# Two scan layers on one Trainium2 core: y kept in DRAM in the order of PSUM's channel blocks, and the second direction of an orientation added by an accumulating DMA

## The chip, the cores and the metric

The kernel runs on one core of a Trainium2 chip. The metric is device time in microseconds (us), the median of three executions. The core has five engines that run beside each other, each with its own queue in program order: PE (matrix multiply; loads of its weights are shown as PEld), DVE (vector), ACT (activations and copies), POOL (GpSimd) and SP (which here only issues DMAs). They meet through semaphores.

## The reference: what is computed

An image batch x of 8 x 64 x 64 x 192 passes two layers; each adds to x the result of a selective scan over the group-normalised x. In one layer:

- `xz = x . in_proj`, split into `xx` and `z`, 384 channels each; `xx` passes a 3 x 3 depthwise convolution and a silu: `xs`, read as a line of L = 4096 positions.
- K directions: layer 0 has two (the line forward and backward, row by row), layer 1 four (row by row and column by column, each forward and backward). For each direction `x_dbl = x_proj . xs` gives dt, B and C; `delta = softplus(dt_proj . dt + bias)`.
- The scan, with 16 states n for each channel d: `h[t] = exp(delta[t] * A) * h[t-1] + delta[t] * xs[t] * B[t]`, `y[t] = sum over n of h[t] * C[t]`; then `y += xs * Ds`.
- The y of all directions are added, each at its own place of the image. Then a layer norm over the channels, times gelu(z) or silu(z), times `out_proj`, plus x.

All of it is in float32.

## The kernel before, in words

Channels stand on the 128 partitions in three tiles (`DT`), so 384 = 3 x 128, and each tile has four blocks of 32 channels (`Q`). The line of an image is cut into 8 chunks of 512 positions (`T`). Each layer has two stages. `front` (L205) makes the normalised x, the convolution and the projections and stores `xs` to DRAM (xcd, row order; xcd_col, column order; xtd, transposed). `scans` (L511) does the rest, and the change lies in it.

**Steps and slots.** `scans` runs over steps: for each image b, each direction k, each chunk c (from the last to the first for a backward direction). Layer 0 has 128 steps, layer 1 has 256. A step has 24 slots (`NSL`): 8 pairs of states m times 3 channel tiles dt. In a slot PE makes `hb` = delta xs B (`inject`, L728) in PSUM, ACT makes `da` = exp(delta A) (`decay`, L745), DVE scans the two states (`scan`, L772, two instructions of 512 positions) into `h`, and POOL multiplies h by C into `hc` (L773). `cr`, which holds C spread over the partitions, is loaded by SP (`load_c`, L714; three buffers). When the three tiles of a pair are done, PE adds `hc` into `py`, a PSUM tile of 128 x 3 x 512, by `reduce` (L780).

**How py is summed.** `block_diag` (L147) multiplies by a 32 x 32 diagonal, four blocks for each tile: block i of tile dt goes to block (i + dt) mod 4 of the partitions. The twelve small multiplications of one state thus use twelve different 32 x 32 places of PE's array and run at the same time. So py holds the channels of tile dt rotated by dt blocks. (In the trace each such multiplication shows as two records, 24 for one state.)

**The order.** It is written out by hand: `at(i, s, f)` puts a helper f at slot s of step i, and slots beyond 24 fall into the next step. `L0_SLOTS` and `L1_SLOTS` (L50, L95) hold the places. Within a slot the scan comes first, then the helpers, then `inject` for two slots later and `decay` for four slots later. Nothing reorders the instructions afterwards.

**y between the directions**, which the change touches:

- k = 0 (first direction): `load_y` at slot 6 loads `xs` (from xcd or xcd_col), and `add_y` (slot 12 in layer 0, 13 in layer 1) adds it to py, times Ds.
- k whose predecessor has the same orientation (layer 0: k = 1; layer 1: k = 1, by columns, and k = 3, by rows): `load_y` loads the y so far from `yrow` or `ycol` in DRAM, and `add_y` adds it by a diagonal of ones.
- layer 1, k = 2, the change from columns to rows: `load_turned` at slots 8 to 19 (L797) loads the chunk's eight rows out of `ycol` in 12 DMAs (3 tiles x 4 parts, runs of 8 numbers, 32 bytes), and `add_y` stands at slot 26.
- `keep_y` at slot 29, which is slot 5 of the next step, copies py to SBUF on ACT (L821) and stores it with five DMAs of SP (L825, L827). Tile 0 goes as it is; tiles 1 and 2 go in two parts each, which turns their blocks back into channel order.

The loaded y, its turned form and the copy of py share one SBUF buffer, called "y" (pool s1, one buffer): each waits for the reader of the one before.

**The final part** (`f_...`) of a finished chunk: `f_load_x` (L836) loads x into `xr`, `f_load` (L850) loads y from `yrow` into `yc`, both at slot 6; then norm, gate (`f_gate`, L871), mean and variance, scale, product with the gate on POOL (`f_times`, L944), output projection (`f_out`, L950). For the images before the last it is spread over the steps of the next image: a chunk every second step in layer 0, every fourth in layer 1. In the last image it comes at once, in the step after the chunk's last direction (`L0_LAST`, `L1_LAST`); there `f_mean` (L888) reads yc from slot 11 (layer 1) or 13 (layer 0) on.

POOL's queue holds the 24 multiplications of a step, two small products for the start of a chunk (`enter`, L665), and the three products of the gate where a chunk is finished. SP's queue holds all loads and stores of the scan stage.

Of the kernel before, what the change touches and what calls it, by code (L numbers as in the profile page):

```python
# [8 lines left out]
F32 = mybir.dt.float32  # L9
AF = mybir.ActivationFunctionType  # L10
ALU = mybir.AluOpType
# [4 lines left out]
P = 128  # L16
B = 8
H = 64
# [5 lines left out]
D = 384  # L24
DT = 3
NS = 16
T = 512
NCH = L // T
RB = T // W
Q = 32  # L30
# [480 lines left out]
def scans(tc, name, x_src, x_dst, xcd, xcd_col, xtd, xdd, t, dirs, rank, row_b, gate, slots, last, consts, dram):  # L511
# [5 lines left out]
    nc = tc.nc  # L517
    ident, mask, grp, mean_w, all_w, eps_gn, eps_ln = consts
    yrow, ycol, cscr, dgd = dram
# [6 lines left out]
    def tiles(a):  # L526
        return a.rearrange("(t p) l -> p t l", p=P)
# [7 lines left out]
    def line(src, c):  # L535
        return src[:, :, c * T : (c + 1) * T]

    steps = []
# [6 lines left out]
    with tc.tile_pool(name=f"{name}_s1", bufs=1) as s1, tc.tile_pool(  # L545
        name=f"{name}_s2", bufs=2
    ) as s2, tc.tile_pool(name=f"{name}_psy", bufs=1, space=PSUM) as psy, tc.tile_pool(
        name=f"{name}_psh", bufs=2, space=PSUM
# [4 lines left out]
        def at(i, s, f, *a):  # L553
            todo.setdefault(i * NSL + s, []).append((f, a))

        live = {}
# [232 lines left out]
        def load_y(i):  # L789

            b, k, cols, rev, ci, c = steps[i]
            y_t = s1.tile([P, DT, T], F32, name="y")
            src = (xcd_col if cols else xcd) if k == 0 else (ycol if cols else yrow)
            nc.sync.dma_start(out=y_t, in_=line(tiles(src[b if k == 0 else b % 2]), c))
            live[i]["y"] = y_t

        def load_turned(i, j):  # L797

            b, k, cols, rev, ci, c = steps[i]
            if j == 0:  # L800
                live[i]["yt"] = s1.tile([P, DT, T], F32, name="y")
                live[i]["y"] = live[i]["yt"].rearrange("p t (w h) -> p t h w", h=RB)
            dt, q = divmod(j, 4)
            cs = slice(q * W // 4, (q + 1) * W // 4)
            nc.sync.dma_start(
                out=live[i]["yt"].rearrange("p t (w h) -> p t w h", h=RB)[:, dt, cs],
                in_=tiles(ycol[b % 2])[:, dt].rearrange("p (w h) -> p w h", h=H)[
                    :, cs, c * RB : (c + 1) * RB
                ],
            )  # L810

        def add_y(i):
            k = steps[i][1]
# [3 lines left out]

        def keep_y(i):
            b, k, cols, rev, ci, c = steps[i]
            y_o = s1.tile([P, DT, T], F32, name="y")  # L820
            nc.scalar.copy(y_o, live[i]["py"])  # L821
            yv = tiles((ycol if cols else yrow)[b % 2])
            for dt in range(DT):
                yd, e = yv[:, dt, c * T : (c + 1) * T], dt * Q
                nc.sync.dma_start(out=yd[: P - e], in_=y_o[e:, dt])  # L825
                if e:
                    nc.sync.dma_start(out=yd[P - e :], in_=y_o[:e, dt])  # L827
            del live[i]


# [137 lines left out]
        def thrice(i, s, f, *a):  # L968
            for p, q in enumerate(s):
                at(i, q, f, *a, p)  # L970

        for i in range(N):
            j = i - 1
            live[i] = {}
            at(j, -3, load_xt, i)
            if xdd is None:
                at(j, -8, load_x, i)
                thrice(j, slots["x_proj"], x_proj, i)
                at(j, slots["x_dbl"], x_dbl, i)
            else:  # L980
                at(j, -4, load_xdbl, i)
            at(j, slots["turn_b"], turn_b, i)
            at(j, slots["keep_b"], keep_b, i)
            for dt in range(DT):
                for f in dt_proj, dt_bias, turn_delta, make_dut:
                    at(j, slots[f.__name__][dt], f, i, dt)
            at(j, slots["softplus"], dt_softplus, i)
            at(j, slots["softplus"] + 1, first_decays, i)
            at(j, 14, enter, i, 0)
            at(j, NSL + 1, enter, i, 1)  # L990
            at(i, -12, load_b, i, 0)
            at(i, 0, load_b, i, 1)
            for m in range(NP):
                at(i, 3 * m - 6, load_c, i, m)
                at(i, 3 * m + 3, carry, i, m)
                for n in range(2):
                    at(i, 3 * m + slots["reduce"][n], reduce, i, m, n)
            b, k, cols, rev, ci, c = steps[i]
            if k and dirs[k - 1][0] != cols:
                for j in range(4 * DT):  # L1000
                    at(i, 8 + j, load_turned, i, j)
                at(i, slots["add_turned"], add_y, i)
            else:
                at(i, 6, load_y, i)
                at(i, slots["add_y"], add_y, i)
            at(i, slots["keep_y"], keep_y, i)

        e = 0
        for b in range(B - 1):
            for c in range(NCH):  # L1010
                e = max(e + K, (b + 1) * K * NCH - NCH + c + 1)
# [19 lines left out]
        for c in range(NCH):  # L1031
            b, e, own = B - 1, N - NCH + c + 1, last
# [34 lines left out]
            for r, fs in enumerate(  # L1067
# [3 lines left out]
                    (dt_proj, turn_b, turn_delta, f_gate, f_mean, f_sum, f_all, f_out, x_proj),  # L1071
                    (reduce, add_y),
                    (load_b, load_c, load_turned),
                )
            )
            for f in fs
        }
        with tc.manual_schedule(engines=ENGINES):
            g = min(todo)
            while todo:  # L1080
                i, s = divmod(g, NSL)
# [11 lines left out]
def vss_layer(tc, name, x_src, x_dst, w, dirs, rank, row_b, gate, slots, last, consts, dram):  # L1093

    with ExitStack() as ctx:
        xcd, xcd_col, xtd, xdd, *dram = dram
        if any(cols for cols, rev in dirs):
            xdd = None
        else:
            xcd_col = None  # L1100
        t = load_weights(tc, ctx, name, w, len(dirs), rank, row_b + 2 * NS, consts[1])
        clear = dram[-1] if xcd_col is None else ()
        front(tc, name, x_src, xcd, xcd_col, xtd, xdd, w["in_proj"][:, :D], t, clear, consts)
        scans(tc, name, x_src, x_dst, xcd, xcd_col, xtd, xdd, t, dirs, rank, row_b, gate, slots, last, consts, dram)
# [99 lines left out]
```

## Time and profile before

| | |
|---|---|
| three runs | 25205.74, 25212.66, 25232.09 us; median 25212.66 |
| profiled execution | span 25231.1 us (the page gives no other time of it), 18.4 above the median and within the three runs |
| scans of layer 0 | 961 to 8928 us |
| scans of layer 1 | 9865 to 25182 us |
| busy share | PE 95%, DVE 93%, POOL 88%, ACT 77% |
| DMA | 4141 MB, 164 GB/s in the mean; SP's queue 61.7% of 16 engines |
| chain that ended last | PE 50%, DVE 25%, ACT 19%, issue 5%, DMA 1% |

Busy time says how long an engine had an instruction running; PE's is modelled for pipelined multiplications. The groups list for each source line the busy time, the mean of one instruction in ns and the idle time of the engine just before it with the releaser that ended most of it. The stretches view gives busy times between two times; here stretches are single steps. The timeline lists instructions in order of time, consecutive ones of a group merged, with the idle time before them in brackets.

### The profile page before, as it was taken

The numbers are of one execution on the slowest core, as the hardware profiler recorded it, in microseconds if no ns is written. First come the engines' busy times: TensorE is split into PE (matmuls) and PEld (weight loads), VectorE is DVE, ScalarE is ACT, GpSimd is POOL, SyncE is SP. The second block draws the span as 40 slices with busy tenths as digits, with TensorE's granted clock in tenths as the row PEclk, the third lists the DMA queues.
The fourth block names the chain that finished last, engine by engine and source line by source line (L and its number), as shares of the span: only waits on it lengthen the run. The fifth ranks groups of instructions, "written<-read, shape, count | busy, mean of one in ns | idle before, by whom it ended". The sixth has DMA issues, their size and how long they took to land.

```text
span 25231.1 us, 794569 instructions
## 1 busy us (share of the span) xinstructions
PE 24024.7 (95%) x340032; PEld 13528.4 (54%) x340032; DVE 23345.8 (93%) x22142; ACT 19452.6 (77%) x37140; POOL 22144.2 (88%) x10287
## 2 busy tenths in 40 slices
PE   9999999999999999999999999999999999999999
PEld 4555555555555544555555555555555555555554
DVE  7899999999999777999999999999999999999998
ACT  5677788778878767777777777777777777777777
POOL 0499999999999713999999999999999999999998
PEclk9999999999999999999999999999999999999999
DMA  4566666666666555675675575675675575576575
GB/s 161 154 158 158 158 158 159 156 158 159 160 158 159 138 179 195 170 164 168 170 166 168 170 165 169 169 165 169 170 163 170 170 164 169 170 163 171 167 166 143
DMA packets 3836413, 4141.15 MB, mean 164 GB/s; under 512 B 2140460, under 2 KB 2340804, under 8 KB 3829828
## 3 DMA queue, kind: packets, MB, share of 16 engines
q1 hardware_dynamic: 3821296, 4032.72, 61.7%
q8 instruction: 2693, 44.12, 0.8%
q10 hardware_dynamic: 11604, 57.59, 0.6%
q14 instruction: 820, 6.72, 0.1%
HBM read 3443.63 MB, written 645.99 MB: 162 GB/s over the span
## 4 chain that ended last, share of the span: by engine, by line
PE 50%; DVE 25%; ACT 19%; issue 5%; DMA 1%; POOL 0%; SPq 0%; DVEq 0%; ACTq 0%; POOLq 0%
DVE h L772 22%; PE hb L728 20%; PE py L151 14%; ACT da L745 8%; PE pt L616 3%; PE pd L568 2%; PE pc L151 2%; PE po L950 2%; PE pz L871 2%; ACT delta L144 2%; ACT L144 1%; ACT L640 1%; PE pi L322 1%; ACT da L753 1%; ACT delta L630 1%
## 5 line engine op out<-in xcount | busy, mean ns | idle before, releaser
L773 POOL TENSOR_TENSOR hc<-h,cr 128x1024 f32<-128x1024 f32 x9216 | 21566.7, 2368 | 2985.7 <-DMA xt_k<-xtd 1844.7
L772 DVE TENSOR_TENSOR_SCAN h<-da,hb 128x512 f32<-128x512 f32 x18432 | 20860.2, 1199 | 1262.2 <-PE hb L728 1038.8
L745 ACT ACTIVATE da<-delta,a_neg 128x512 f32<-128x512 f32 x18432 | 12249.7, 713 | 1763.7 <-DVE h L772 1736.3
L728 PEld LDWEIGHTS hb<-dg,dut 64*128 64x128 f32 x147456 | 9215.4, 185 | 6720.3 <-issue 5785.3
L728 PE MATMUL hb<-dg,dut 64*128 64x128 f32 x147456 | 10835.6, 286 | 603.9 <-DVE h L772 413.0
L151 PE MATMUL py<-hc,mask 32*32 32x512 f32 x147456 | 6866.8, 601 | 36.0 <-ACT y L821 32.7
L151 PEld LDWEIGHTS py<-hc,mask 32*32 32x32 f32 x147456 | 1582.8, 103 | 2359.7 <-issue 1722.2
L753 ACT COPY da<-a 128x2 f32<-128x2 f32 x8064 | 1562.5, 194 | 293.9 <-ACT da L745 1.8
L778 ACT COPY st<-h 128x6 f32<-128x6 f32 x2688 | 537.4, 200 | 1142.3 <-DVE h L772 1140.0
L616 PE MATMUL pt<-xdbl,w_dt 96*128 96x512 f32 (+1 forms) x2304 | 1302.2, 646 | 38.8 <-DVE yc L914 15.9
L630 ACT ACTIVATE delta<-pt,dtb 128x512 f32<-128x512 f32 x1152 | 787.2, 683 | 449.5 <-PE pt L616 444.4
L355 DVE SCALAR_TENSOR_TENSOR tp<-pad,cw,tp 128x512 f32<-128x512 f32 x1344 | 988.2, 750 | 113.0 <-ACT tp L349 78.9
L683 PE MATMUL pq<-ident,delta 128*128 128x128 f32 x4608 | 758.7, 287 | 324.4 <-DVE dut L691 226.6
L871 PE MATMUL pz<-xn_sq,w_in 96*128 96x512 f32 x1536 | 835.3, 643 | 42.0 <-ACT g L882 27.2
L691 DVE TENSOR_TENSOR dut<-pq,xt_k 128x512 f32<-128x512 f32 x1152 | 767.7, 666 | 83.4 <-PE pq L683 83.4
L568 PE MATMUL pd<-x_k,w_x 128*128 128x512 f32 x1536 | 798.3, 629 | 35.8 <-DVE yc L914 15.1
L950 PE MATMUL po<-yc,w_out 128*96 128x512 f32 x1536 | 783.0, 621 | 16.2 <-POOL yc L944 13.3
L683 PEld LDWEIGHTS pq<-ident,delta 128*128 128x128 f32 x4608 | 484.2, 141 | 522.0 <-DVE dut L691 342.9
L151 PE MATMUL pc<-pad,taps 32*32 32x512 f32 x13824 | 577.9, 592 | 17.1 <-ACT xo L370 13.4
L821 ACT COPY y<-py 128x1536 f32<-128x1536 f32 x384 | 551.7, 1437 | 35.7 <-PE py L151 19.4
L144 ACT ACTIVATE delta<-delta 128x1536 f32<-128x1536 f32 x384 | 570.4, 1485 | 4.3
L944 POOL TENSOR_TENSOR yc<-yc,g 128x512 f32<-128x512 f32 x384 | 490.0, 1279 | 79.1 <-ACT yc L935 72.9
(105 smaller groups left out, 10143.1 us busy)
## 6 DMA issues: line engine op xcount, KB each, us to landing
cr<-cscr SPq DMA_DIRECT2D x2048, 512.0 KB, 4.4
dg<-dgd SPq DMA_DIRECT2D x1536, 512.0 KB, 7.9
cr<-xdd SPq DMA_DIRECT2D x1024, 512.0 KB, 6.4
xt_k<-xtd SPq DMA_DIRECT2D x768, 384.0 KB, 7.1
xcd<-xo SPq DMA_DIRECT2D x128, 768.0 KB, 3.5
xtd<-xv SPq DMA_DIRECT2D x128, 768.0 KB, 4.4
y<-yrow SPq DMA_DIRECT2D x128, 768.0 KB, 5.0
yc<-yrow SPq DMA_DIRECT2D x128, 768.0 KB, 7.2
```

What stands on the lines that cost most here:

```text
L144: nc.scalar.activation(out, in_, AF.Softplus)
L151: nc.tensor.matmul(out[j * Q : (j + 1) * Q, dt], w[i * Q : (i + 1) * Q], x[i * Q : (i + 1) * Q], start=first, stop=last, tile_position=(i ...
L568: nc.tensor.matmul(live[i]["pd"][:R], w_x[:, dt, k, :], live[i]["x"][:, dt], start=(dt == 0), stop=(dt == DT - 1),)
L616: nc.tensor.matmul(pt, w_dt[:, k, dt * P : (dt + 1) * P], live[i]["xdbl"][:rank], start=True, stop=True,)
L683: nc.tensor.transpose(pq[:, g], live[i]["delta"][:, dt, g * P : (g + 1) * P], ident)
L728: nc.tensor.matmul(hv[:, r, q], live[i]["dut"][r * G : (r + 1) * G, dt, q], dg[r * G : (r + 1) * G, q, :, 2 * mm : 2 * mm + 2], start=True ...
L745: nc.scalar.activation(da[:, n].rearrange("p (r g j) -> p r g j", r=2, j=G), live[i]["delta"][:, dt].rearrange("p (g r j) -> p r g j", r=2 ...
L753: nc.scalar.copy(da[:, :, f], live[i]["a0"][:, dt, 2 * m : 2 * m + 2])
L772: nc.vector.tensor_tensor_scan(o, a, v, init, ALU.mult, ALU.add)
L773: nc.gpsimd.tensor_mul(hc[:, dt], h[:, dt], live[i]["cr", m])
L871: nc.tensor.matmul(fin["pz"], w_in[:, u, dt * P : (dt + 1) * P], fin["xn"][:, u], start=(u == 0), stop=(u == CT - 1),)
L950: nc.tensor.matmul(fin["po"][:CP], w_out[:, dt, u * CP : (u + 1) * CP], fin["y"][:, dt], start=(dt == 0), stop=(dt == DT - 1),)
```

## The change

Four things:

- `keep_y` only copies; a new `store_y` writes the three tiles with **one** DMA, in the order in which PSUM holds them. So `yrow` and `ycol` hold tile dt rotated by dt blocks.
- In a step whose predecessor direction has the same orientation (`same`), nothing is loaded and no `add_y` is made. `store_y` comes a slot later (slot 30, which is slot 6 of the next step) and goes through GpSimd's queue as a DMA that adds to what DRAM holds (`accum_op=ALU.add`). These are 64 + 128 = 192 steps. The other 192 store with SP.
- `load_turned` must turn the blocks back for `block_diag`: for tiles 1 and 2 each part is loaded in two DMAs (96 + 32 or 64 + 64 partitions). 20 DMAs instead of 12.
- The final part's weights are laid out for channels that are rotated once more (`ry`: 2 dt blocks).

```diff
@@ load_y @@
-            src = (xcd_col if cols else xcd) if k == 0 else (ycol if cols else yrow)
-            nc.sync.dma_start(out=y_t, in_=line(tiles(src[b if k == 0 else b % 2]), c))
+            nc.sync.dma_start(out=y_t, in_=line(tiles((xcd_col if cols else xcd)[b]), c))
@@ load_turned @@
-            nc.sync.dma_start(
-                out=live[i]["yt"].rearrange("p t (w h) -> p t w h", h=RB)[:, dt, cs],
-                in_=tiles(ycol[b % 2])[:, dt].rearrange("p (w h) -> p w h", h=H)[
-                    :, cs, c * RB : (c + 1) * RB
-                ],
-            )
+            yt = live[i]["yt"].rearrange("p t (w h) -> p t w h", h=RB)[:, dt, cs]
+            yd = tiles(ycol[b % 2])[:, dt].rearrange("p (w h) -> p w h", h=H)[
+                :, cs, c * RB : (c + 1) * RB
+            ]
+            e = dt * Q
+            nc.sync.dma_start(out=yt[: P - e], in_=yd[e:])
+            if e:
+                nc.sync.dma_start(out=yt[P - e :], in_=yd[:e])
@@ keep_y @@
-            y_o = s1.tile([P, DT, T], F32, name="y")
-            nc.scalar.copy(y_o, live[i]["py"])
-            yv = tiles((ycol if cols else yrow)[b % 2])
-            for dt in range(DT):
-                yd, e = yv[:, dt, c * T : (c + 1) * T], dt * Q
-                nc.sync.dma_start(out=yd[: P - e], in_=y_o[e:, dt])
-                if e:
-                    nc.sync.dma_start(out=yd[P - e :], in_=y_o[:e, dt])
+            live[i]["yo"] = s1.tile([P, DT, T], F32, name="y")
+            nc.scalar.copy(live[i]["yo"], live[i]["py"])
+
+        def same(i):
+            k, cols = steps[i][1:3]
+            return k > 0 and dirs[k - 1][0] == cols
+
+        def store_y(i):
+            b, k, cols, rev, ci, c = steps[i]
+            y_d = line(tiles((ycol if cols else yrow)[b % 2]), c)
+            if same(i):
+                nc.gpsimd.dma_start(out=y_d, in_=live[i]["yo"], accum_op=ALU.add)
+            else:
+                nc.sync.dma_start(out=y_d, in_=live[i]["yo"])
             del live[i]
@@ the places @@
-            else:
+            elif k == 0:
                 at(i, 6, load_y, i)
                 at(i, slots["add_y"], add_y, i)
             at(i, slots["keep_y"], keep_y, i)
+            at(i, slots["keep_y"] + 1 * same(i), store_y, i)
@@ the weights of the final part @@
+    ry = np.concatenate([np.roll(rx[dt], 2 * dt, axis=0).reshape(-1) for dt in range(DT)])
...
-            "in_proj": np.concatenate([g("in_proj_w")[:D], g("in_proj_w")[D:][rx]]).T,
+            "in_proj": np.concatenate([g("in_proj_w")[:D], g("in_proj_w")[D:][ry]]).T,
-            "out_proj": g("out_proj_w").T[rx],
+            "out_proj": g("out_proj_w").T[ry],
```

The layer norm's weights (`ln_w`, `ln_b`) take `ry` in the same way.

More of the change, by code (lines that the diff above doesn't have):

```diff
@@ L1184 @@
             "dt_b": by_part(g("dt_projs_bias")[ko][:, rx], 1),
-            "ln_w": by_part(g(lw)[rx], 0),
-            "ln_b": by_part(g(lb)[rx], 0),
+            "ln_w": by_part(g(lw)[ry], 0),
+            "ln_b": by_part(g(lb)[ry], 0),
             "Ds": by_part(g("Ds").reshape(K, D)[ko][:, rx], 1),
```

## The prediction, made before the changed kernel ran

> **What bounds the kernel.** I began with the busy times and the costliest groups.
>
> ```profile
> PE 24024.7 (95%) x340032; PEld 13528.4 (54%) x340032; DVE 23345.8 (93%) x22142; ACT 19452.6 (77%) x37140; POOL 22144.2 (88%) x10287
> ...
> L773 POOL TENSOR_TENSOR hc<-h,cr 128x1024 f32<-128x1024 f32 x9216 | 21566.7, 2368 | 2985.7 <-DMA xt_k<-xtd 1844.7
> L772 DVE TENSOR_TENSOR_SCAN h<-da,hb 128x512 f32<-128x512 f32 x18432 | 20860.2, 1199 | 1262.2 <-PE hb L728 1038.8
> ```
>
> Three engines are nearly full and pass work to each other slot by slot, so a mean share decides nothing. I therefore cut the second layer into steps, by the stretches view. In layer 1 a finished chunk is normalised and projected every fourth step, so four steps make a round; these four (direction k=1, which the change touches) repeat almost to the nanosecond. Columns: the stretch, its length, busy time of PE, PEld, DVE, ACT, POOL.
>
> ```profile
> 16014.78:16075.85 61.07, 59.90 (x849) 32.87 (x839) 58.56 (x56) 43.95 (x77) 60.49 (x29) 1.00 0.56 156
> 16075.85:16136.91 61.06, 58.30 (x832) 32.13 (x828) 56.02 (x53) 47.29 (x96) 56.44 (x27) 1.00 0.65 187
> 16136.91:16194.28 57.37, 55.54 (x846) 31.31 (x828) 55.68 (x53) 45.59 (x93) 56.51 (x27) 1.00 0.60 166
> 16194.28:16252.05 57.77, 55.63 (x828) 31.58 (x828) 57.17 (x54) 49.15 (x96) 56.12 (x27) 1.00 0.58 165
> ```
>
> POOL is idle for 0.58, 4.62, 0.86 and 1.65 us: 7.7 us in a round. That is the room for anything new on it. No row gives one bound: the short steps hang on DVE and POOL, the long ones on bursts of PE.
>
> **Part 1, the removed add.** 192 steps lose the add of y: 24 matmul records, 1.11 us of PE each, 213 us in all. What it is worth is seen from a step that already lacks it: in k=2 the add stands at slot 26, not 13. First DVE, then PE, around slots 13 to 15 of a k=1 step, from the timeline:
>
> ```profile
> 16112.54 0.67 DVE L691 TENSOR_TENSOR dut<-pq,xt_k 128x512 f32<-128x512 f32 x1
> 16114.64 2.33 DVE L772 TENSOR_TENSOR_SCAN h<-da,hb 128x512 f32<-128x512 f32 x2 [1.44 <-ACT st L778]
> ```
>
> ```profile
> 16112.26 1.11 PE L151 MATMUL py<-y,mask 32*32 32x512 f32 x24
> 16113.31 1.19 PE L728 MATMUL hb<-dg,dut 64*128 64x128 f32 x16
> ```
>
> and DVE at the same slots of the k=2 step:
>
> ```profile
> 16589.26 0.67 DVE L691 TENSOR_TENSOR dut<-pq,xt_k 128x512 f32<-128x512 f32 x1
> 16590.32 2.33 DVE L772 TENSOR_TENSOR_SCAN h<-da,hb 128x512 f32<-128x512 f32 x2 [0.40 <-PE hb L728]
> ```
>
> The hole before the scan is 1.44 us with the add and 0.40 without: 1.04 us. In the other three steps of a round the scans of slots 13 to 16 keep the same pace in k=1 and k=2, so there the add is hidden behind DVE. Gain: k=1 and k=3, 8 images, 2 rounds each, less the 2 of the last image: 30 x 1.04 = **-31 us**. In layer 0 nothing is late after the add at slot 12:
>
> ```profile
> 4536.42 0.67 DVE L691 TENSOR_TENSOR dut<-pq,xt_k 128x512 f32<-128x512 f32 x1
> 4537.00 4.54 DVE L772 TENSOR_TENSOR_SCAN h<-da,hb 128x512 f32<-128x512 f32 x4
> ```
>
> DVE runs without a hole, so 64 adds there are worth 0.
>
> **Part 2, the accumulating DMA on POOL.** 192 instructions, each placed after the multiplication of slot 6, with 24 multiplications of 2.37 us per step queued around it. It waits for ACT's copy of y, which ends at 16150.5 in the third step above, while POOL gets there at about 16156: no wait. Its time X on POOL is not in this trace. From below, SP issues a 768 KB load in 0.39 us; from above, the five SP issues that now write the same 384 runs of 2 KB take 0.79 + 0.44 + 0.48 + 0.60 = 2.31 us (timeline of SP at 24914.57). I take X = 2.0, near the second row, since each run must be described and this DMA also reads its destination; both ends are kept.
>
> The price comes from the lag. The third and fourth steps and the next round's first have 0.86 + 1.65 + 0.58 = 3.1 us idle against 3X; only then comes the step with 4.62. POOL already runs up to 3.1 us behind the scans in slots 8 to 12 of the first step (one multiplication of the gate in the way). It may lag by three slots of 2.22 less its own 2.34 = 4.3 us before a scan finds its h buffer unread. So a round pays 3X - 3.1 + 3.1 - 4.3 = 3X - 4.3: at X = 2.0, 1.7 us; 32 rounds make **+54 us**; at 0.39 it is 0, at 2.31 +84. In layer 0 the gaps are larger (62.79 us steps with 59.44 busy): 0.
>
> The Trainium skill, "DMA: Bandwidth & Descriptors", section "Latency and other measured facts", gives about 1 us to the first byte of a GpSimd DMA and names the Q7's emission as the reason. By that, as an estimate, this term would be 0 and the sum 54 us lower.
>
> The multiplications range only from 2.334 to 2.461 us while DVE is 96% busy beside them, so nothing on DVE shuts GpSimd out here. The skill's "SBUF — State Buffer", section "SBUF: two separate sides", speaks against the change: GpSimd cannot write descriptors while DVE runs a two-port operation, and a DMA of 620 ns then takes 3100. The sum would be 104 us higher if that held for every one.
>
> **Part 3, SP's loads behind the new write.** A load that needs the accumulated y, or its buffer, now waits for POOL's multiplication, X and the landing. Landing: 3.5 (768 KB from SBUF, xcd<-xo) to 7.2 us (yc<-yrow); I take 5.0, as y<-yrow. Such loads come about 7 us later: 14 f_load of a first chunk, 14 load_y after a last step, 8 load_turned. Behind each, SP's next cr load is held; it is issued 12.5 us before POOL needs it and lands in 4.4, so 8 us are free: 0. In the last image every chunk is read at once, and there it costs. Layer 1: f_load goes at 24922.1 + 2.0 + 5.0 = 24929.1 instead of 24921.64, lands 7.2 later at 24936.3, and this reader stands in PE's queue before it:
>
> ```profile
> 24931.56 1.13 PE L888 MATMUL pm<-yc,mean_w 128*128 128x512 f32 x2
> ```
>
> 4.7 us late in 7 steps, less the add of 1.11 that these full steps save: **+25 us** (0 to +66 for X and landing at their ends and beyond). Layer 0's last image goes the other way. There ACT waits for x:
>
> ```profile
> ACT xn_sq L859 <- DMA xr<-x: 35.2, 7, 6.1
> ```
>
> because SP issues that load only after five stores and a load of y that waits for them:
>
> ```profile
> 8464.34 0.81 SPq L825 DMA_DIRECT2D yrow<-y  x2
> ...
> 8469.58 0.38 SPq L794 DMA_DIRECT2D y<-yrow  x1
> 8470.02 0.48 SPq L836 DMA_DIRECT2D xr<-x  x1
> ```
>
> Without them it goes at about 8462.4, and the whole wait is covered. Next late are cr loads behind the held f_load, about 2 us, on a POOL that is idle a quarter of these steps: **-30 us** (-35 to 0).
>
> **Part 4, load_turned in 20 pieces instead of 12** (64 steps). From slot 12 on SP is never free in a k=2 step, mostly because an issue is held until earlier 32-byte runs have moved; the runs stay the same. An issue that is not held takes 0.43 us. The last piece and its reader now:
>
> ```profile
> 16668.65 0.44 SPq L805 DMA_DIRECT2D y<-ycol  x1
> ```
>
> ```profile
> 16674.37 2.44 PE L151 MATMUL py<-y,mask 32*32 32x512 f32 x24
> ```
>
> With 4.5 us to land, 1.2 us are spare. Eight more issues cost between 0 and 3.4 us; I take 1.5, nearer to "held anyway": 0.3 x 64 = **+20 us** (0 to +141).
>
> At nothing: four of the five stores and 192 loads that leave SP (SP waits for POOL's cr buffers anyway, 34 of 57 us in the third step above), the weights in another order, and the other k=0 stores.
>
> **Sum.** -31 + 54 + 25 - 30 + 20 = +38 us on the profiled execution's span of 25231.1. That span is 18.4 above the median of 25212.66 and within the three runs; 38 on the median gives **25250 us**.
>
> **Rivals.** *Slower:* GpSimd's issue is dearer. One mechanism, POOL's room in layer 1; it begins to cost at X = 1.4 (3X = 4.3), 96 us for each us beyond, and makes the kernel slower by over 50 us from X = 2.1, where the other terms' -16 are outweighed. At X = 3.0 the term is 150, the sum +134: 25347. For it: POOL's idle time above. Against: nothing measured. *Faster:* X at or below 1.4, a short landing, pieces of load_turned free: -31 - 35 + 5 = -61, 25152. Its extreme, PE as the only bound, would give 213 us: 25000; the pair of DVE rows above speaks against it. *Landing far longer than 5 us,* since the destination is read and written: the 36 held loads use up their 8 us, up to 36 us for each us beyond, besides 7 for each in the last image. At 15 us: about +110 more, 25360. *The change does not do what it says:* y's single buffer could hold back the next copy until the write has landed; but that copy comes a step (57 us) later, so this needs a landing no row suggests.
>
> **Chances.** The forecast (within 0.2%, 50 us, about what a measurement of this kernel can tell from no change) 0.40; dear issue, long landing or dear pieces, slower by more, 0.41; cheap issue, faster by more, 0.19. The range reaches from the faster rival, 25150, to the slower ones with room for the pieces, 25400.
>
> **What would show it.** X: the DMA rows on POOL's queue and the gap between multiplications there. Part 1: the 1.44 us hole gone in 30 steps and nothing gained in layer 0's plain steps. Part 3: L859's 35 us gone in layer 0, a new wait of PE's mean for yc in layer 1's last image. Part 4: a wait of PE's add for y in k=2 steps. I would be wrong if POOL's gap exceeded 2.3 us, or if scans sped up in steps where POOL has no room.

## The result, and the profile after

Measured beside the kernel before on one chip: before 25216.39 us (median of 17 runs, 25199.23 to 25232.09), after **25268.47 us** (17 runs, 25247.5 to 25305.13). The ratio is 1.0022, with a 95% interval of 1.0015 to 1.0029: 52 us slower at the medians, 0.2%. The forecast was 25250.

The profiled execution of after has a span of 25252.6 us and a time of 25254.87, near the low end of its runs; that of before lay near the high end of its own. So the two traces differ by 21.5 us where the medians differ by 52, and where the time went is read slot by slot. For that I took the time from the first scan of one slot to the first scan of the next in both traces, and summed the differences over the steps that do the same:

| place | steps | forecast, us | measured, us |
|---|---|---|---|
| layer 1, k=1 and k=3, slot 14 of a round's second step (the add's hole) | 30 | -31 | -29.2 |
| layer 1, the other slots of k=1 and k=3 (POOL's room) | | +54 | about 0 |
| layer 1, last image | 8 | +25 | +39.3 |
| layer 0, last image | 8 | -30 | -21.3 |
| layer 1, k=2 and the first step behind it (the turned load) | 72 | +20 | +52 |
| sum | | +38 | +41 |

The sum is right and four of its terms are not. Two small differences stand in no row: behind the last scan of each layer after is 2.3 and 5.5 us longer.

The 120 steps of layer 0 ahead of its last image make -26 more in this pair, at irregular slots. I give that to no part of the change: kernels below that leave layer 0 as it is (`e1`, `e2`, `e6`, `e11`) stand 5 to 36 us above after's profile in the same steps. What differs there is PE's granted clock, which the traces record as 1.0 or 0.5. Between the first scans of step 0 and of step 120 it is halved for 84 us in before and for 35 us in after. Over all 13 profiles here, the length of these steps (7320 to 7356 us) goes with the time at half clock in them (33 to 87 us): the correlation is 0.95, with 0.58 us of length for each us at half clock. Why the clock drops there more often in one profile than in another is open. Before is the only one of the 13 with all 64 adds of y in layer 0, and it lies 4 us below that line, within the scatter of the others (7 us), so these adds show no cost.

The first lines of after's page, busy times and the two costliest groups:

```profile
PE 23878.2 (95%) x335424; PEld 13491.2 (53%) x335424; DVE 23350.6 (92%) x22142; ACT 19427.1 (77%) x37140; POOL 22346.5 (88%) x10479
...
L773 POOL TENSOR_TENSOR hc<-h,cr 128x1024 f32<-128x1024 f32 x9216 | 21680.0, 2499 | 2800.3 <-DMA xt_k<-xtd 1843.0
L772 DVE TENSOR_TENSOR_SCAN h<-da,hb 128x512 f32<-128x512 f32 x18432 | 20865.7, 1200 | 1268.9 <-PE hb L728 1121.2
```

PE lost 146 us of work and the kernel as a whole is no faster; POOL has 192 instructions more, and its multiplications keep it busy 113 us longer in all. Now the four steps of after that answer to those shown of before (length, then PE, PEld, DVE, ACT, POOL):

```profile
15984.66:16045.73 61.07, 58.86 (x824) 32.64 (x814) 58.56 (x56) 43.94 (x77) 60.49 (x29) 1.00 0.49 141
16045.73:16105.74 60.01, 57.25 (x808) 31.94 (x804) 56.01 (x53) 47.11 (x96) 57.59 (x28) 1.00 0.67 178
16105.74:16163.13 57.39, 54.60 (x827) 31.12 (x804) 55.67 (x53) 45.51 (x93) 57.34 (x28) 1.00 0.58 152
16163.13:16220.92 57.79, 54.64 (x804) 31.41 (x804) 57.20 (x54) 49.12 (x96) 56.95 (x28) 1.00 0.58 152
```

Only the second is shorter, by 1.05 us; the other three lose 1 us of PE's work each and keep their length to 0.02. POOL in the third is idle for 0.05 us instead of 0.86, and nothing waits for it. In the second step the hole ahead of DVE's scan is closed:

```profile
16082.43 0.67 DVE L691 TENSOR_TENSOR dut<-pq,xt_k 128x512 f32<-128x512 f32 x1
16083.49 2.33 DVE L772 TENSOR_TENSOR_SCAN h<-da,hb 128x512 f32<-128x512 f32 x2 [0.40 <-PE hb L728]
```

What POOL pays for the accumulating DMA, from its timeline in the fourth step:

```profile
16174.25 9.35 POOL L773 TENSOR_TENSOR hc<-h,cr 128x1024 f32<-128x1024 f32 x4
16183.55 1.23 POOL L833 DMA_DIRECT2D ycol<-y  x1
16184.37 12.11 POOL L773 TENSOR_TENSOR hc<-h,cr 128x1024 f32<-128x1024 f32 x5
```

The row says 1.23 us (1.28 in the median of 192), but the next multiplication starts 0.82 after it and runs beside its end. That multiplication takes 2.87 us instead of 2.37. Both together, X is **1.3 us**, not 2.0. The multiplications behind it have rows as long (about 2.8 us until POOL's next idle time), but each starts 2.33 us after the one before, as ever: the rows overlap, and the 0.5 us is paid once for a DMA. That is why the mean of all rows rises by 131 ns and the busy time by only 113 us.

And the landings, from after's list of DMA issues (number, size, median us from the start of the row to the landing):

```profile
yrow<-y SPq DMA_DIRECT2D x128, 768.0 KB, 4.8
yrow<-y POOLq DMA_DIRECT2D x128, 768.0 KB, 7.9
...
ycol<-y POOLq DMA_DIRECT2D x64, 768.0 KB, 8.0
```

8 us, where the forecast had 7.0 from the same point (X of 2.0 and a landing of 5.0). Who waits for it shows in the waits of PE and of SP in after (us in all, times, longest). In before PE waited for yc once, for 4.6 us, SP at the load of yc for 1.3 us in all, and the other two waits weren't there. Of the 8 waits for yc in after, 7 (27.1 us) are in layer 1's last image and one (3.8 us) in layer 0's:

```profile
PE pm L896 <- DMA yc<-yrow: 30.9, 8, 6.2
...
PE py L151 <- DMA y<-ycol: 8.3, 4, 3.8
```

```profile
SPq L858 <- DMA yrow<-y: 425.2, 30, 17.5
...
SPq L809 <- DMA ycol<-y: 68.0, 8, 8.9
```

The last row was the clue: eight times, once in each image, SP stands 8.5 us at the *first piece of the turned load*, since that load reads all columns and the last column chunk lands late. I had counted the cr loads behind it and not the pieces themselves. PE's timeline in the second k=2 step of the third image shows the end of that chain:

```profile
14605.37 2.29 PE L151 MATMUL py<-y,mask 32*32 32x512 f32 x16
14609.12 2.27 PE L151 MATMUL py<-y,mask 32*32 32x512 f32 x8 [1.46 <-DMA y<-ycol]
14611.33 2.08 PE L728 MATMUL hb<-dg,dut 64*128 64x128 f32 x16
14613.33 2.29 PE L568 MATMUL pd<-x_k,w_x 128*128 128x512 f32 x4
14615.56 1.19 PE L728 MATMUL hb<-dg,dut 64*128 64x128 f32 x16
```

The wait is 1.46 us, and then `hb` takes 2.08 us instead of 1.19. In the stretches view, whose seventh number is the granted clock of PE, the first line below is the stretch behind this wait, the second that behind a wait of 3.07 us for yc in layer 1's last image:

```profile
14609.12:14613.33 4.21, 4.21 (x24) 2.09 (x24) 0.00 (x0) 0.66 (x2) 2.44 (x2) 0.67 0.89 270
...
24928.77:24932.52 3.75, 3.75 (x42) 1.99 (x41) 0.00 (x0) 3.69 (x11) 2.35 (x1) 0.54 0.98 324
```

Each holds one stretch of 3.41 us at a clock of 0.5; a us or two is lost in it. So in these places a wait of PE costs its length and then that slower clock. The Trainium skill, "TensorE: Matmul & The Clock Gate", section "What's actually happening", gives PE half its clock after an idle window of about 3.4 us; these rows show the halved clock already behind recorded waits of 1.46 and 3.07 us.

### The profile page after: what moved, and what is told of

It reads as the page before. It is cut to its first block, busy times and chain, and to the rows that moved or that the text cites. A ratio compares the mean times of both kernels' runs of the same rounds, so it can differ in the third digit from the quotient of the medians.

```text
span 25252.6 us, 783478 instructions
## 1 busy us (share of the span) xinstructions
PE 23878.2 (95%) x335424; PEld 13491.2 (53%) x335424; DVE 23350.6 (92%) x22142; ACT 19427.1 (77%) x37140; POOL 22346.5 (88%) x10479
## 4 chain that ended last, share of the span: by engine, by line
PE 31%; DVE 16%; ACT 11%; issue 4%; DMA 1%; POOL 1%; SPq 0%; DVEq 0%; ACTq 0%; POOLq 0%
DVE h L772 15%; PE hb L728 13%; PE py L151 9%; ACT da L745 5%; PE pd L568 2%; PE pt L616 2%; PE pz L879 1%; PE pc L151 1%; PE po L958 1%; ACT delta L144 1%; POOL hc L773 1%; ACT L144 1%; ACT L640 1%; ACT y L822 1%; ACT da L753 1%
## 5 line engine op out<-in xcount | busy, mean ns | idle before, releaser
L616 PE MATMUL pt<-xdbl,w_dt 96*128 96x512 f32 (+1 forms) x2304 | 1300.3, 645 | 39.9 <-DVE yc L922 16.1
L879 PE MATMUL pz<-xn_sq,w_in 96*128 96x512 f32 x1536 | 835.0, 643 | 28.9 <-ACT g L890 25.8
L568 PE MATMUL pd<-x_k,w_x 128*128 128x512 f32 x1536 | 799.8, 630 | 36.2 <-DVE yc L922 15.1
L822 ACT COPY y<-py 128x1536 f32<-128x1536 f32 x384 | 549.9, 1432 | 28.8 <-PE py L151 21.1
```

What stands on the lines that cost most here:

```text
L568: nc.tensor.matmul(live[i]["pd"][:R], w_x[:, dt, k, :], live[i]["x"][:, dt], start=(dt == 0), stop=(dt == DT - 1),)
L616: nc.tensor.matmul(pt, w_dt[:, k, dt * P : (dt + 1) * P], live[i]["xdbl"][:rank], start=True, stop=True,)
L879: nc.tensor.matmul(fin["pz"], w_in[:, u, dt * P : (dt + 1) * P], fin["xn"][:, u], start=(u == 0), stop=(u == CT - 1),)
```

## The experiments

All are edits of the changed kernel, but `e7`, which is one of the kernel before. The median of the kernel before was 25224.63 us beside `e1` to `e4`, 25224.29 beside `e5` to `e8`, and 25222.2 beside `e9` to `e11`; differences are against these, and after's own difference is +52. An interval of a ratio is about 20 us to either side here, so terms of 10 to 25 us are read from the traces, slot by slot. Those scatter too: the second k=2 steps of `e2`, which that edit leaves alone, are 9 us longer than after's.

**e1_halves: the turned load in 12 pieces again.**

```diff
-            cs = slice(q * W // 4, (q + 1) * W // 4)
-            nc.sync.dma_start(out=yt[: P - e], in_=yd[e:])
-            if e:
-                nc.sync.dma_start(out=yt[P - e :], in_=yd[:e])
+            if dt == 0:
+                cs, to, src = slice(q * W // 4, (q + 1) * W // 4), slice(0, P), slice(0, P)
+            else:
+                half, part = divmod(q, 2)
+                cs = slice(half * W // 2, (half + 1) * W // 2)
+                to = slice(P - e, P) if part else slice(0, P - e)
+                src = slice(0, e) if part else slice(e, P)
+            nc.sync.dma_start(
+                out=live[i]["yt"].rearrange("p t (w h) -> p t w h", h=RB)[to, dt, cs],
+                in_=tiles(ycol[b % 2])[src, dt].rearrange("p (w h) -> p w h", h=H)[
+                    :, cs, c * RB : (c + 1) * RB
+                ],
+            )
```

> The changed kernel, but load_turned takes tiles 1 and 2 in halves of the columns instead of quarters, so a chunk comes in 12 DMAs again (4 + 4 + 4) with the same 32-byte runs at the same slots. My theory (the pieces): the step-by-step comparison puts +48 us into the k=2 steps, 29 of them in the slot after the late add of the round's first step; the number of DMAs that SP issues is what makes the last piece late, so these steps come back to the kernel before within 10 us, and the median falls from 25268 to about 25220 (25205 to 25235). Rival (the accumulating writes are still under way, or the rows are read more slowly because they were written by the accumulation): the k=2 steps keep their +48 us and the median stays at 25268 within 12 us.

25243.58 us (25230.73 to 25274.15, 11 runs), ratio 1.0009 (1.0000 to 1.0018): +19. In the trace, k=2 and the step behind it give back 18 of the 52 us, nearly all of it in the first, third and fourth steps of the rounds. The second steps stay as long as they were: +28.9 against before, where after has +30.1. So the pieces cost about 18, near the 20 of the forecast, and most of the 30 us there has another cause.

**e2_last_sp: layer 1's last 8 steps load y, add it by identity multiplications, and store by SP.**

```diff
-            return k > 0 and dirs[k - 1][0] == cols
+            return k > 0 and dirs[k - 1][0] == cols and not late(i)
+        def late(i):
+            return K == 4 and i >= N - NCH
@@ add_y @@
+                if late(i):
+                    nc.tensor.matmul(live[i]["py"][:, dt], ident, live[i]["y"][:, dt], start=False, stop=False)
+                    continue
@@ the places @@
-            elif k == 0:
+            elif k == 0 or late(i):
```

> The changed kernel, but in the last 8 steps (layer 1, last image, last direction) y is loaded and added as before and stored by SP without accumulation; the add there is made by three full multiplications with the identity, since yrow holds PSUM's order (about 1.98 us of PE, as x_dbl's three, instead of 1.11). My theory (yc comes late): PE's mean no longer waits for yc, the +39 us of these steps fall to about +7 x 0.9 = +6, and the median falls from 25268 to about 25236 (25225 to 25250). Rival (the loss of these steps is the lowered clock or the order of SP's loads, not the landing of the accumulating write): they keep more than 25 us and the median stays above 25255.

25242.3 us (25230.12 to 25259.67, 11 runs), ratio 1.0009 (1.0000 to 1.0018): +18. The trace gives back 27.4 us in layer 1's last image. The rest of its 39 is the adds that came back (1.7 us more at slot 14 in the median).

**e3_three: each accumulating DMA issued as three, one for each tile.**

```diff
-                nc.gpsimd.dma_start(out=y_d, in_=live[i]["yo"], accum_op=ALU.add)
+                for dt in range(DT):
+                    nc.gpsimd.dma_start(
+                        out=y_d[:, dt], in_=live[i]["yo"][:, dt], accum_op=ALU.add
+                    )
```

> The changed kernel, but each accumulating DMA is issued as three, one for each channel tile: same bytes, three times the fixed part of GpSimd's issue. In the changed kernel one issue holds POOL for about 1.3 us, under the 1.4 us from which I worked out a loss. My theory (POOL's room in layer 1): with X between 2.4 and 3.9 us a round loses 3X - 4.3, so 32 rounds lose 93 to 237 us, most of it in k=1 and k=3 steps of layer 1, and the median rises from 25268 to between 25360 and 25505. Rival (POOL's issue is not what counts, only the landing and the loads that wait for it): the median rises by less than 25 us.

25352.72 us (25340.31 to 25363.42, 5 runs), ratio 1.005 (1.0036 to 1.0064): +128. POOL in the step that answers to the fourth above:

```profile
16217.35 9.75 POOL L773 TENSOR_TENSOR hc<-h,cr 128x1024 f32<-128x1024 f32 x4
16226.63 3.10 POOL L834 DMA_DIRECT2D ycol<-y  x3
16228.32 20.06 POOL L773 TENSOR_TENSOR hc<-h,cr 128x1024 f32<-128x1024 f32 x8
```

From multiplication 6 to 7 it is 3.99 us instead of 2.33, and the latter takes 3.41 instead of 2.37: X is 2.7. Now POOL's room is used up, at the place where the prediction put it: slot 11 of a round's first step is longer, and these steps take 75 us more than in after, 2.4 in each of the 31 rounds that follow four accumulating steps. In that step of k=1 the multiplication of slot 11 starts 3.10 us behind the end of its scan in before, 4.05 in after and 5.69 here (medians); then the scan is held. The lag may thus grow to 5.7 us, where I had worked out 4.3. The formula 3X - 4.3 gives 3.8 a round at this X; 2.4 fits 3X - 5.7. The mechanism stands, and its threshold is X = 1.9, not 1.4. The lag also bears out X: three DMAs less the 3.1 us of idle time are 0.8 us in after, where the lag grows by 0.95, and 5.0 here, where it grows by 2.6 and 2.4 are held.

**e4_sp_plain: the same store, plain, by SP** (the sum of the two directions is left out).

```diff
-                nc.gpsimd.dma_start(out=y_d, in_=live[i]["yo"], accum_op=ALU.add)
+                nc.sync.dma_start(out=y_d, in_=live[i]["yo"])
```

> The changed kernel, but the second direction's y is stored by SP as a plain DMA at the same slot: it overwrites the first direction's y instead of being added to it (the sum of the two directions of an orientation is left out). It takes away GpSimd's issue and the accumulation, and keeps the missing add, the single store and the 20 pieces. My theory (GpSimd's issue is free, its landing costs only in layer 1's last image): the median falls by the 39 us of these steps and a few us more, from 25268 to about 25225 (25210 to 25240), and the k=1 and k=3 steps of layer 1 outside the last image change by less than 8 us in sum. Rival (the issue on POOL or the traffic of the accumulation costs everywhere): the median falls below 25195, with the difference spread over the k=1 and k=3 steps.

25184.15 us (25166.65 to 25191.39, 11 runs), ratio 0.9981 (0.9973 to 0.9990): -40, below what my theory allowed. It had only the 39 us of layer 1's last image. The trace has those (-39.3) and two more places: layer 0's last image -18.1, and the second k=2 step of each image -22.7. The plain steps of k=1 and k=3 do not change (-2.8 and +0.3). So the time falls in three places, and none of it where POOL is full. In layer 1's last image and at the turned load, 62 us in all, something waits for the landing. In layer 0's last image it is PE's clock: halved for 41 us of these steps in after and for 7 us here. That is no price of GpSimd's DMA: `e7`, which has none, stands where after does (-19.9, 44 us at half clock).

**e5_pool_plain: plain, but by GpSimd** (the sum of the two directions is left out).

```diff
-                nc.gpsimd.dma_start(out=y_d, in_=live[i]["yo"], accum_op=ALU.add)
+                nc.gpsimd.dma_start(out=y_d, in_=live[i]["yo"])
```

> The changed kernel with the same DMA on GpSimd's queue, but one that overwrites instead of adding (left out: the sum of an orientation's two directions). What costs in the changed kernel is, by its trace and the run with SP's plain store (92 us less than the changed kernel), that a store by GpSimd lands late: layer 1's last image (39 us), layer 0's last image (18 us), and the first chunk of the turned load (23 us), which SP can't start before the last column chunk has landed. Theory A: it is late because adding takes the DMA longer (8.0 us against 4.8 for SP's plain store); then this kernel keeps only the later start on POOL's queue (about 2 us) and is at 25195 to 25225 on a kernel before of 25216. Rival B: it is late because of GpSimd's issue and queue, whatever the DMA does; then the landing stays near 8 us and the time at 25245 to 25270. The gap between POOL's multiplications of slots 6 and 7 (3.13 us against 2.33 without a DMA) should stay under both if the issue makes it, and shrink under A if adding makes it.

25216.19 us (25177.45 to 25236.64, 11 runs), ratio 0.9996 (0.9987 to 1.0005): -8, within theory A's range, but not for its reasons alone: the medians are 60 us apart and the places that the theory names give back 38 in the trace. Its POOL and its landings:

```profile
16206.48 0.81 POOL L833 DMA_DIRECT2D ycol<-y  x1
16207.31 14.01 POOL L773 TENSOR_TENSOR hc<-h,cr 128x1024 f32<-128x1024 f32 x6
```

```profile
yrow<-y POOLq DMA_DIRECT2D x128, 768.0 KB, 4.8
...
ycol<-y POOLq DMA_DIRECT2D x64, 768.0 KB, 4.4
```

The gap between multiplications 6 and 7 stays at 3.13 us: it does not come from adding. Adding makes the row longer (1.28 against 0.81), lengthens the next multiplication (here it keeps its 2.37) and adds 3 to 3.6 us to the landing. Layer 1's last image loses 32.8 of its 39 us without the adding, so there the landing decides. Layer 0's last image gives back nothing (+1.4; its clock is halved for 44 us). The second k=2 step loses only 6.9 of 23: there it is mostly the start. In the third image SP stores the last column chunk 14.72 us into the step (`e4`), POOL, which runs behind the scans, 22.02 (after) and 22.03 (here), and the first turned piece follows at 21.25, 29.98 and 27.97.

**e6_turn_sp: only the last column chunk of each image goes by SP**, with the edit of `e2`, load at slot 10, add at slot 24, and

```diff
+            return K == 4 and steps[i][1] == 1 and steps[i][4] == NCH - 1
```

> The changed kernel, but the last chunk of direction k=1 of each image in layer 1 (8 steps) loads the y so far, adds it by three identity multiplications at slot 24 and is stored by SP as a plain write. Theory: the extra 28.6 us at slot 1 of the second k=2 step of each image (16 steps of two rounds, nearly all of it in the 8 that follow a change from columns to rows) come from SP, which holds the first piece of the turned load until the accumulating DMA of the last column chunk has landed (68 us of waiting, 8 times). Then this kernel loses about 23 us against the changed kernel: 25235 to 25255 on a kernel before of 25216, with the surplus gone in those 8 steps and the 20 pieces' cost (0.3 to 0.4 us in the other 56 steps) left. Rival: the surplus there is of the 20 pieces too; then the time stays at 25260 to 25275.

25278.21 us (25242.04 to 25301.6, 11 runs), ratio 1.002 (1.0011 to 1.0029): +54, as slow as after, so the number I gave was missed. The trace shows why: the second k=2 step loses 23.3 us and SP's wait at the turned load is gone, as the theory says, but the add, done at slot 24 = slot 0 of the next step, makes the first k=2 step 1.8 us longer, 15.2 in all. The cause was right; this cure costs two thirds of it.

**e7_no_add: the kernel before without the load and the add in the 192 steps** (that sum is left out).

```diff
-            else:
+            elif k == 0:
                 at(i, 6, load_y, i)
                 at(i, slots["add_y"], add_y, i)
```

> The kernel before without the load of y and its addition in the 192 steps whose predecessor has the same orientation (left out: that sum); its five stores, order of y and 12 pieces stay. This is the first part of the change alone, with SP's loads. Theory: 30 steps lose a hole of 1.04 us (31 us), layer 0's last image loses the wait of ACT for x (21 to 35 us), the rest of the 213 us of PE is hidden: 25150 to 25175 on a kernel before of 25216. Rival: PE is the bound in most steps, and a good part of 213 us is gained: 25000 to 25100.

25159.62 us (25153.0 to 25170.65, 9 runs), ratio 0.9975 (0.9965 to 0.9985): -65, in the middle of the first range. The trace gives -29.4 in k=1 and k=3 and -19.9 in layer 0's last image. The rest of the 65 is not placed: layer 0's plain steps are 19.4 us shorter than in before's profile, and at half clock for 54 us, where before has 84. Of 213 us of PE's work, 29 are seen on the path; a bound by PE alone is out.

**e8_mix: `e1`, and SP with identity adds in the last 8 steps of both layers and in the last column chunks.**

```diff
+            return i >= N - NCH or (K == 4 and steps[i][1] == 1 and steps[i][4] == NCH - 1)
```

> The changed kernel with three edits: the turned load in 12 pieces (tiles 1 and 2 in halves of columns), the last 8 steps of both layers, and the last chunk of direction k=1 of each image in layer 1, load y (slot 10), add it by identity multiplications (slot 24) and are stored by SP as a plain write. Theory: the costs are separate waits in separate steps, so the gains add up: 20 for the pieces, 34 for layer 1's last image, 23 for the held turned load, up to 18 for layer 0's last image, which leaves 25165 to 25200 on a kernel before of 25216, faster than both kernels. Rival: the loads that come back hold SP where the late landing did, above all the loads of x in layer 0's last image (30 us there); then 25195 to 25235.

25229.79 us (25225.41 to 25256.39, 11 runs), ratio 1.0005 (0.9996 to 1.0014): +6; my sum was missed, and the rival's range holds it. Against after's trace: the second k=2 step -28.6 and the first +13.1 (the add again), layer 1's last image -21.1 of 39, layer 0's last image +4.9. In layer 0 it is not the loads of x, which the rival named: slot 1, where the identity add now stands, grew by 15.1 us (2.7 in most steps), and slots 3 and 12 lost 8.9. An add put back on a full PE takes most of what the earlier landing gives.

That suggested moving things instead, with nothing put back.

**e10_early: the store one slot earlier.**

```diff
-            at(i, slots["keep_y"] + 1 * same(i), store_y, i)
+            at(i, slots["keep_y"], store_y, i)
```

> The changed kernel with one edit: the accumulating store stands at slot 29, not 30, so that it starts one multiplication (2.3 us) earlier on GpSimd's queue. Theory: what waits for the landing gains up to 2.3 us each: 16 in 7 steps of layer 1's last image, 14 in 7 of layer 0's, 10 to 18 in the 8 steps after a held turned load; together 25 to 48 below the changed kernel, 25220 to 25245 on a kernel before of 25220. Rival: GpSimd then waits for ACT's copy with its multiplications queued behind; then no gain, or a loss: 25265 to 25300.

25254.43 us (25242.12 to 25258.83, 11 runs), ratio 1.0012 (1.0004 to 1.0021): +32, 20 below after and short of the 25 to 48. The trace has a hit and two misses. Layer 1's last image: -29.2, more than the 16 worked out: PE's wait for yc falls by 15.7 us, and the time at half clock behind the waits goes from 30.7 to 6.8 us. Layer 0's last image: -3.9. The turned load: -1.2. There the store now starts at 19.70 us instead of 22.02, and the first piece goes at 29.70 instead of 29.98, because the landing grew with the lead:

```profile
yrow<-y POOLq DMA_DIRECT2D x128, 768.0 KB, 9.4
...
ycol<-y POOLq DMA_DIRECT2D x64, 768.0 KB, 9.6
```

1.5 of the 2.3 us are lost in the transfer (medians). What it shares the DMA engines with, I did not try.

**e11_turn_later: the add of the turned y two slots later in the first k=2 step.**

```diff
-                at(i, slots["add_turned"], add_y, i)
+                at(i, slots["add_turned"] + 2 * (ci == 0), add_y, i)
```

> The changed kernel with one edit: the add of the turned y stands at slot 26, not 24, in the first step of direction k=2 (8 steps). Theory: it is the held first turned load that made the second k=2 step longer (28.6 us at its slot 1, 8 times); two slots later the pieces have landed, and 20 us of it go without any add elsewhere: 25240 to 25255 on a kernel before of 25220. Rival: something behind that add (the last reduction and the copy of py) is as late; then 25260 to 25275.

25272.26 us (25258.73 to 25294.91, 11 runs), ratio 1.0021 (1.0012 to 1.003): +50; the median does not show the 20 us. The trace does: the second k=2 step loses 19.1 us (-34.6 at slot 1, +21.0 at slot 3, where the add now stands). But this profile is 36 us longer than after's in the plain steps of layer 0, which the edit does not touch; PE is at half clock for 86 us of them, in after for 35. By the medians alone the edit's worth stays open.

**e9_best: `e1`, `e10` and `e11` together, and the first mean of y of layer 1's last image wholly at slot 12** (`f_mean` from (11, 12, 12) to (12, 12, 12)).

> The changed kernel with four edits that move things and bring no load of y back: the turned load in 12 pieces (tiles 1 and 2 in halves of columns); the store of a step at slot 29, beside the copy, and not at 30, also on GpSimd; the add of the turned y at slot 26, not 24, in the first step of direction k=2; the mean of y in layer 1's last image from slot 12 on, not 11. Theory: the time was lost in three waits for a late landing and to the 20 pieces, each in its own steps, and each is covered by being moved: 20 for the pieces, 20 to 25 for the held turned load, 25 to 39 in layer 1's last image, up to 14 in layer 0's; 25165 to 25200 on a kernel before of 25220, faster than both kernels. Rival: GpSimd reaches the store at slot 5 before ACT's copy is done and waits there, with its multiplications behind it, in every round (1 us or more in 32 rounds); then 25215 to 25260.

**25193.96 us** (25176.37 to 25221.36, 11 runs), ratio 0.9990 (0.9981 to 0.9999): -28, faster than both kernels, as expected, though the interval ends just short of 1. Against after's trace: k=2 and the step behind it -40 of 52, layer 1's last image -36.9 (all but 2.4), layer 0's last image -4.3. PE's wait for y in the k=2 steps is gone, and for yc it is down to

```profile
PE pm L901 <- DMA yc<-yrow: 11.0, 4, 4.4
```

The same add of the turned y as above in PE's timeline, now at slot 2, in one piece and with `hb` at 1.20 us:

```profile
14603.33 1.20 PE L728 MATMUL hb<-dg,dut 64*128 64x128 f32 x16
14604.45 1.11 PE L151 MATMUL py<-hc,mask 32*32 32x512 f32 x24
14605.33 1.66 PE L151 MATMUL py<-y,mask 32*32 32x512 f32 x12
```

## Why the prediction was right, and where its steps were not

The time was 18 us above the forecast, and the profiled pair's sum of terms is +41 against +38. But the forecast got there partly by luck, through errors that cancel: one term was 54 too high, three others 55 too low together.

- **Part 1, the removed add:** right in size and place, -29.2 for -31, in 30 steps at slot 14 and nowhere else in layer 1; `e7` gives -29.4 by itself. One slip in its text: in layer 1 the turned add stands at slot 24, not 26, which is layer 0's number (the description of the kernel before has the same slip); the reading of the hole doesn't hang on it.
- **Part 2, "I take X = 2.0, near the second row":** the term that failed in size. X is 1.3: the row of 1.28, of which 0.46 lies beside the next multiplication, and 0.5 by which that one is longer. At that X the term is nothing, and +54 becomes 0. The mechanism was right: at X = 2.7 (`e3`) POOL's lag ends at slot 11 of a round's first step, as worked out, with 1.4 us more room in a round than I gave it. Of the two rules weighed there, that of the Trainium skill's "SBUF — State Buffer", section "SBUF: two separate sides" (3100 ns a DMA where GpSimd is shut out), is not what these rows show: their median is 1.28 us, the longest 3.58. (By the formula it would have added 106 us, not 104.) The other, about 1 us to the first byte, would have given this term its right size, 0; the time to the first byte itself is not read from any run here.
- **Part 3, "Landing: ... I take 5.0":** with X before it the forecast had 7.0 us from the start of POOL's row, and it is 8.0; `e5` shows that adding makes 3 to 3.6 us of it. The load of yc behind it was quicker than forecast (4.7 and 4.9 us where its landing is on record in the middle steps, not 7.2). So in layer 1's last image the wait I named is there, in about the size of the term: PE's mean waits 27.1 us for yc in 7 steps. The place costs 39.3 and not 25, since PE's clock is lower after each wait, which no term held: it is halved for 30.7 us of these steps, and never there in before or with the wait gone (`e2`, `e4`).
- **Part 3, layer 0's last image:** ACT's wait for x went as forecast, and "next late are cr loads" came true as well. SP issues x early, then stands at yc until the sum has landed, and the cr loads queue behind it:

```profile
8513.56 0.45 SPq L844 DMA_DIRECT2D xr<-x  x1
8529.17 0.36 SPq L858 DMA_DIRECT2D yc<-yrow  x1
8529.62 5.11 SPq L714 DMA_DIRECT2D cr<-xdd  x3
```

  POOL then waits for cr 7 times in these steps, 16.1 us in all (never in before), and that costs little, as assumed: in `e7`, which has no such wait, the steps are no shorter. The size is what failed, -21.3 of -30: the 35.2 us of waits went, but not all of them were on the path. Where the steps reach -39.4 (`e4`), it is PE's clock that differs: halved for 6.8 us, in after for 41.0, in before for 54.6. Half of the 34 us between after and `e4` is 17 of the 18 us between their steps. Why the clock stays up in `e4` is open.
- **Part 3, "the 36 held loads ... 8 us are free: 0":** no cost of 28 of them shows (layer 1's k=0 steps differ by +1.0 us in all), but it was wrong for the 8 turned loads. Their own pieces were late, not the cr loads behind them: the first piece goes 8.6 us later than before, 7.3 of it by the later start on POOL's queue, and I had given the last piece 1.2 us to spare. About 23 us (`e4` -22.7, `e6` -23.3, `e11` -19.1).
- **Part 4, the 20 pieces:** +20 forecast, 18 by `e1`; 28 are left in k=2 and the step behind it under `e4`, where the first piece is not held.

The faster rival named X at or below 1.4 together with a short landing and free pieces; only the first came. The rival of a far longer landing named the held loads, and 8 of them did cost, at a landing of 8 us and not of 15. What stays open is why PE's clock in the plain steps of layer 0 drops more often in one execution than in another, which is worth some 30 us between profiles, and so whether anything of the 52 us at the medians is beyond the +41 of the terms.

## What to carry to other kernels

When a store is replaced by an accumulating DMA, don't stop at the engine that issues it. List everything that reads the destination, and for each reader add the later place in the queue, the longer landing and what PE loses after the wait; the readers that need *all* of it, like a transposing load, come first. Waits that follow are cheaper to cover by moving the reader or the store by a slot or two (`e9`) than by putting the old work back on a full engine (`e6`, `e8`).

## What the runs showed of the hardware

- A row of a DMA on POOL's queue is not the time that it takes from POOL. The next multiplication starts 0.46 us before the row ends; it is longer by 0.5 us if the DMA adds (2.87 against 2.37) and not at all if it overwrites (2.37). The rows behind it are as long after an adding DMA, but overlap: they start 2.33 us apart. The Trainium skill, "Perfetto Trace Analysis", section "DMA Instruction — SWDGE (GPSIMD)", says that such a row ends when the descriptors are written and not when the data has moved; the landing 7.9 to 8.0 us after the issue, beside a row of 1.28, agrees.
- Adding costs 3 to 3.6 us of landing for 768 KB (7.9 and 8.0 against 4.8 and 4.4 us, both issued by GpSimd), and the same DMA started one slot earlier landed only 0.8 us earlier in the median (9.4 and 9.6 us).
- Three accumulating DMAs of 256 KB hold POOL for 2.7 us in all, twice as long as one of 768 KB.
- A short wait of PE (1.46 or 3.07 us) was followed by some 4 us at a mean granted clock of 0.67 or 0.54. In all 13 traces the clock is recorded as 1.0 or 0.5, and the stretches at 0.5 last 3.41 us or a multiple of it (but for the one at the trace's end). They account for most of the 36 us by which the plain steps of layer 0 differ between profiles.
